# Two column blocks of a gated projection take two of their five later products together, by seven half-width products

## The chip, the cores and the metric

The kernel runs on one core of one Trainium2 chip. The metric is the device time of one execution in microseconds (us), as the median of several runs. The engines are named as in the profile: PE is TensorE, PEld its weight loads, DVE VectorE, ACT ScalarE, POOL GpSimd and SP SyncE.

## The reference

A graph network over 1024 nodes with 512 features: a graph convolution, four layers of attention and gated feed-forward, and a second graph convolution. All of it is float32. The change lies in the gated feed-forward of each layer:

```python
for i in range(L):                                   # L = 4
    a = _attn(_ln(h, ln2_w[i], ln2_b[i]), cond, Wq[i], Wk[i], Wv[i], Wo[i])
    h = h + a
    u = _ln(h, ln3_w[i], ln3_b[i]) @ geglu_w[i] + geglu_b[i]      # 512 -> 4096
    val, gate = jnp.split(u, 2, axis=-1)
    f = val * jax.nn.gelu(gate, approximate=False)                # 1024 x 2048
    h = h + f @ ffo_w[i] + ffo_b[i]                               # 2048 -> 512
```

## The kernel before

**Products by sevens.** Most matrix products are split into two by two blocks and made from seven block products instead of eight, with sums of left blocks and of right blocks formed beforehand on POOL or DVE, and sums of the results formed on DVE. The seven are numbered 0 to 6. Products 0 and 1 go into one bank of PSUM (a), product 5 into b, 6 and then 3 into c, 4 and then 2 into d. Product 3 is accumulated onto product 6 in c, and so it can begin only when DVE has read product 6 out of c; product 2 waits in the same way for the read of product 4 in d.

**The gated projection.** The 2048 hidden columns are made in four quarters, the loop over `r`. In a quarter the left side is weights (four blocks of 256 rows and 512 columns: values and gates, upper and lower half) and the right side the turned, normalised activations `ln3T` with their sums `ln3S`. The 512 hidden columns of a quarter are four column blocks of 128, `c` = 0 to 3.

- Quarters 1 to 3 use `Pair` (L1074): each of the products 0, 5, 6 and 4 is split into seven once more, for the column blocks `p` and `p + 2` together, in `InStep.seven_of` (L1012). The inner left sums `gi` and the inner right sums `gr` are made on POOL.
- Quarter 0, where the activations are only just ready, uses `Quad` (L930), one object per column block. `first` and `second` make products 0 and 1 during the end of the attention. `rest` (L956) makes the other five, 5, 6, 4, 3, 2 in this order, each as two matmuls of 128x512 (`multiply`, L298), with one DVE operation or two after each. ACT applies Gelu to both gates. The value rows `fT` follow on DVE, L975 to L978.

`geglu` (L1185) calls `rest` of the four blocks one after the other, then `beside(c)`, then `sums(c)`, which makes the left sums `fT`/`fs` of the following output projection on DVE (L1191 to L1195). `beside` issues, for c = 0 and 1, the right sums `gr` on POOL for the products 0, 5, 6, 4 of the later quarters, and for c = 2 the weight sums `wffs` of the output projection, four DVE operations (L214 to L217). After that `ffn_out` (L1215, banks `fa` to `fd`) runs the output projection, and POOL waits for the last `fs` (`geglu.last`) and makes the weight sums `ges` and the inner left sums `gi` of quarter 1.

Ahead of quarter 0 POOL adds the bias of the output projection to six of the eight row blocks of `h` (`add_bias`, L1505), behind the last sums of the activations.

The inner seven as it stands in `seven_of`, for two products side by side in one bank, each step two matmuls of 128x256 per product:

```python
product(0, a, True);   nc.scalar.copy(s1, a)
product(5, b, True);   add(halves_of(u2), b, s1)
product(6, c, True);   add(halves_of(s1), c, u2)
product(4, d, True);   add(w[1][:, :, M:], d, s1)
product(1, a, False);  nc.scalar.copy(w[0][:, :, :M], halves_of(a))
product(3, c, False);  add(w[1][:, :, :M], c, u2)
product(2, d, False);  self.last = add(w[0][:, :, M:], d, u2)
```

**What sets the order.** Each engine works off its own queue in order. A scheduler in the recording layer places the instructions of each engine by dependencies, due times and pool rooms when the program is built; `tc.issue_after` and `tc.keep_in_program_order` bind it, and `waiting_for` adds a wait. PSUM has eight banks, handed out from one pool.

Of the kernel before, what the change touches and what calls it, by code (L numbers as in the profile page):

```python
# [17 lines left out]
P = 128  # L18
# [5 lines left out]
def gnn_kernel(  # L24
# [70 lines left out]
    def t512(name, dtype=F32):  # L95
        return work.tile([P, 512], dtype, tag="t512", name=name)
# [4 lines left out]
    def slots_of(n, name):  # L101
        return [slot(f"{name}_{i}") for i in range(n)]
# [598 lines left out]
    def acc_tile(name):  # L701
        return accs.tile([P, 512], F32, tag="acc", name=name)
# [204 lines left out]
    def order7(blk, s1, s2, s4):  # L907

        return [blk[0], blk[1], s4, blk[3], s1, s2, blk[2]]
# [13 lines left out]
    def out_weights(t, l, r, wff):  # L923
        s = slots_of(2, f"wffs_{l}_{r}")
        b11, b12, b21, b22 = (wff[k][:, :, d * M:(d + 1) * M] for k in range(2) for d in range(2))
        t1, t2, t4 = (halves_of(s[i // 2][:, i % 2, :]) for i in range(3))
        sums_of_b(t, b11, b12, b21, b22, t1, t2, t4)
        return [b11, b21, b22, t4, t1, t2, b12]

    class Quad:  # L930
# [5 lines left out]
            self.cv = l * 2 * DFF // P + r * KC + c  # L936
            self.left, self.right = left, right

        def product(self, i, to, start):
            multiply(to, self.left[i], self.right[i],  # L940
                     [(self.c * P, (self.c + 1) * P, 0, 512)], start)

        def first(self):
            self.a = bank(f"ga_{self.n}")
# [9 lines left out]
            nc.scalar.activation(pre, pre, AF.Gelu, bias=gcols[:, cg:cg + 1])  # L954

        def rest(self):  # L956
            n, c, bias = self.n, self.c, gcols[:, self.cv:self.cv + 1]
# [6 lines left out]
            nc.vector.tensor_tensor(u3, pc, u2, OP.add)  # L964
            self.product(4, pd, True)
            g1 = t512(f"g1_{n}")
            nc.vector.tensor_tensor(g1, pd, u3, OP.add)
            self.gate(g1, n)
            self.product(3, pc, False)
            g0 = t512(f"g0_{n}")  # L970
            nc.vector.tensor_tensor(g0, pc, u2, OP.add)
            self.gate(g0, n)
            self.product(2, pd, False)
            v1 = acc_tile(f"gv1_{n}")
            nc.vector.scalar_tensor_tensor(v1, pd, bias, u2, OP.add, OP.add)  # L975
            f0, f1 = (self.fT[i][c // 2][:, c % 2, :] for i in range(2))
            nc.vector.tensor_tensor(f1, v1, g1, OP.mult)
            return lambda: nc.vector.scalar_tensor_tensor(f0, self.a, bias, g0, OP.add, OP.mult)  # L978

    def inner_left(t, x, s1, s2, s4):  # L980

# [5 lines left out]
    def quarters(room):  # L987
        return [room[:, k, j * M:(j + 1) * M] for k in range(2) for j in range(2)]
# [14 lines left out]
    def inner_right_of(i, right, rooms):  # L1003
        return inner_right(nc.gpsimd, *quarters(right[i]), rooms)
# [69 lines left out]
    class Pair(InStep):  # L1074
# [47 lines left out]
    class KeyPair(InStep):  # L1122
# [43 lines left out]
        def final(self, q, d):  # L1166
            nc.scalar.copy(self.to(0, q, 1), halves_of(d))

    def cond_rights(l, g):

        rooms = slots_of(4, f"kr_{l}_{g}")
        of = conds[l, g], conds[l, g + 1]
        return {i: inner_right(nc.gpsimd, *(x[i][:, k, :] for k in range(2) for x in of), quarters(room))
                for i, room in zip(INNER[0] + INNER[1], rooms)}

    def pairs_of(l, r, left, right, inner):
        fT = [slots_of(2, f"fT_{l}_{r}_{i}") for i in range(2)]
        return (fT, slots_of(3, f"fs_{l}_{r}"),
                [Pair(l, r, p, left, right, inner, fT) for p in range(2)])
# [5 lines left out]
    def geglu(quads, fT, s, begun, beside=lambda c: None):  # L1185
        def sums(c):
            k = c % 2
            a11, a12, a21, a22 = (fT[i][j][:, k, :] for i in range(2) for j in range(2))
            s1, s2, s4 = (x[:, k, :] for x in s)
            if c < 2:  # L1190
                nc.vector.tensor_tensor(a21, a11, a21, OP.subtract)  # L1191
            else:
                nc.vector.tensor_tensor(s2, a22, a21, OP.subtract)
                nc.vector.tensor_tensor(s1, s2, a11, OP.add)
                sums.last = nc.vector.tensor_tensor(s4, a12, s2, OP.subtract)  # L1195

        made = []

        def sums_of_made():
            while made:  # L1200
                sums(made.pop(0))

        for c, q in enumerate(quads):
            if begun:
                q.last = q.rest()()
                beside(c)
# [226 lines left out]
    for l in range(L):  # L1433
# [211 lines left out]
        last = l == L - 1  # L1645
        lnT = None
        kept = slot(f"kept_{l}")
        rights = {}

        for r in range(R):  # L1650
            if r:
                wff = out_weights(nc.gpsimd, l, r, raw_out)
            else:
                raw_out = load_out(l, 0)
            if r + 1 < R:
                raw = load_geglu(l, r + 1)
            beside = lambda c: None
            if r:
                fT, fS, quads = pairs_of(l, r, left, right, (lefts, rights))
            else:  # L1660
                wff = []

                rooms = slots_of(4, f"gr_{l}")
# [9 lines left out]
            fT = geglu(quads, fT, fS, not r, beside)  # L1673
            if r + 1 < R:
                raw_out = load_out(l, r + 1)
                with waiting_for(geglu.last, mybir.EngineType.Pool):
                    left = geglu_weights(l, r + 1, *raw)
                    rooms = [t512(f"gi_{l}_{r + 1}_{i}") for i in range(6)]
                    lefts = inner_lefts(left, [x[:, i * M:(i + 1) * M] for x in rooms
                                               for i in range(2)])  # L1680
                for s in range(2):
                    ffn_out(l, r, s, fT, wff, kept)
            elif last:
                w_out, base, again, dinv_row = load_last()
                with waiting_for(geglu.last, mybir.EngineType.Pool):
                    for nb in range(NB - 2, NB):
                        add_bias(nb)
                    w_out = out_weights(nc.gpsimd, L, 0, w_out)
                ffn_out(l, r, 0, fT, wff, kept)
            else:  # L1690
                lnT = [slots_of(2, f"ln2T_{l + 1}_{i}") for i in range(2)]
                projections = load_projections(l + 1, add_bias)
                ffn_out(l, r, 0, fT, wff, kept)
                ready_first(l + 1, [0, 1, 4, 5])
                ffn_out(l, r, 1, fT, wff, kept)
                turn_first(l + 1, [0, 1, 4, 5])
                left_to_turn = [2, 3, 6, 7]
                ready_first(l + 1, left_to_turn[:2])
# [144 lines left out]
```

## Time and profile before

| | |
|---|---|
| median of 3 runs | 2458.13 us (2458.05 to 2458.39) |
| profiled execution, its own time | 2458.91 us |
| its span, first to last instruction | 2457.1 us |
| PE busy | 2437.9 us, 99% of the span |
| DVE busy | 1584.0 us, 64% |
| ACT busy | 725.0 us, 30% |
| POOL busy | 920.3 us, 37% |
| granted TensorE clock, mean | 0.999 |

A row of the timeline gives the start in us from the span's start, the duration from the start of the first merged instruction to the modelled end of the last, the engine, the line, the operation, out<-in, the shape and the number of merged instructions; in brackets stands how long the engine had been idle and what ended that. The profile shows a float32 matmul as two records, so one product of two matmuls shows as x4. PE's records overlap, since matmuls are pipelined: the price of a matmul is the distance from start to start, not the duration of its row. The windows view gives busy time and count (x) of each engine in a stretch.

### The profile page before, as it was taken

The numbers are of one execution on the slowest core, as the hardware profiler recorded it, in microseconds if no ns is written. First come the engines' busy times: TensorE is split into PE (matmuls) and PEld (weight loads), VectorE is DVE, ScalarE is ACT, GpSimd is POOL, SyncE is SP. The second block draws the span as 40 slices with busy tenths as digits, with TensorE's granted clock in tenths as the row PEclk, the third lists the DMA queues.
The fourth block names the chain that finished last, engine by engine and source line by source line (L and its number), as shares of the span: only waits on it lengthen the run. The fifth ranks groups of instructions, "written<-read, shape, count | busy, mean of one in ns | idle before, by whom it ended". The sixth has DMA issues, their size and how long they took to land. (4 is left out here: it accounts for less than half of the span.)

```text
span 2457.1 us, 34452 instructions
## 1 busy us (share of the span) xinstructions
PE 2437.9 (99%) x13032; PEld 1881.7 (77%) x13032; DVE 1584.0 (64%) x3240; ACT 725.0 (30%) x1616; POOL 920.3 (37%) x1059
## 2 busy tenths in 40 slices
PE   7999999999999999999999999999999999999999
PEld 5778886677787887577787888477777888667777
DVE  9665666566676557666686557666685656666674
ACT  7323343122213334122213334222223333322230
POOL 0334433632553223533633224444524222454421
PEclk9999999999999999999999999999999999999999
DMA  6323222110212221111212222011131031111120
GB/s 180 121 69 116 91 95 69 52 35 18 103 31 78 88 70 59 35 52 35 77 56 69 78 71 76 18 52 52 35 99 69 14 125 44 61 52 52 37 93 35
DMA packets 78892, 163.50 MB, mean 67 GB/s; under 512 B 6952, under 2 KB 15472, under 8 KB 78720
## 3 DMA queue, kind: packets, MB, share of 16 engines
q1 hardware_dynamic: 76624, 155.81, 19.1%
q0 software_dynamic: 1376, 4.30, 0.5%
q8 instruction: 107, 1.75, 0.3%
q10 hardware_dynamic: 720, 1.11, 0.1%
q14 instruction: 65, 0.53, 0.1%
HBM read 138.12 MB, written 23.07 MB: 66 GB/s over the span
## 5 line engine op out<-in xcount | busy, mean ns | idle before, releaser
L221 POOL TENSOR_TENSOR ges<-wgate,wgate 128x1024 f32<-128x1024 f32 x16 | 37.7, 2355 | 443.2 <-DVE fs L1195 401.3
L797 ACT ACTIVATE pr<-sc,nmax 128x256 f32<-128x256 f32 x256 | 118.2, 471 | 85.5 <-DVE nmax L792 85.0
L298 PE MATMUL pa_v<-wv,ct 128*128 128x256 f32 x512 | 123.9, 385 | 0.0
L298 PE MATMUL fa<-wff,fT 128*128 128x256 f32 x512 | 121.6, 379 | 0.0
L298 PE MATMUL pc_v<-wv,ct 128*128 128x256 f32 x512 | 121.0, 379 | 0.0
L298 PE MATMUL pd_v<-wvs,ct 128*128 128x256 f32 x512 | 121.0, 379 | 0.0
L994 POOL TENSOR_TENSOR kr<-ct,ct 128x256 f32<-128x256 f32 x48 | 36.7, 765 | 211.8 <-DVE pr L802 207.2
L298 PEld LDWEIGHTS fa<-wff,fT 128*128 128x128 f32 x512 | 97.3, 190 | 21.8 <-issue 9.6
L1029 ACT COPY gs<-ga 128x512 f32<-128x512 f32 x48 | 27.9, 582 | 287.7 <-PE ga L1022 287.7
L298 PEld LDWEIGHTS pa_v<-wv,ct 128*128 128x128 f32 x512 | 94.9, 190 | 22.5 <-issue 9.2
L792 DVE TENSOR_REDUCE nmax<-sc 128x2 f32<-128x512 f32 x128 | 83.6, 678 | 41.2 <-PE sc L785 41.2
L298 PEld LDWEIGHTS pd_v<-wvs,ct 128*128 128x128 f32 x512 | 97.3, 190 | 13.2
L298 PEld LDWEIGHTS pc_v<-wv,ct 128*128 128x128 f32 x512 | 97.0, 190 | 13.0
L298 PE MATMUL ga<-ln3T,wval 128*128 128x512 f32 x224 | 104.4, 594 | 0.0
L1103 ACT ACTIVATE g<-g,gcols 128x512 f32<-128x512 f32 x96 | 69.3, 722 | 94.5 <-DVE g L1100 94.5
L802 DVE TENSOR_SCALAR pr<-pr,inv 128x256 f32<-128x256 f32 x256 | 78.3, 348 | 2.9
L894 POOL TENSOR_TENSOR ou<-ou 128x256 f32<-128x256 f32 x12 | 8.7, 726 | 190.5 <-DVE ou L893 127.4
L1230 DVE TENSOR_TENSOR hall<-fd,hall 128x512 f32<-128x512 f32 x64 | 44.1, 689 | 52.1 <-PE fd L298 52.1
L298 PE MATMUL gc<-ln3S,wgate 128*128 128x512 f32 x160 | 75.2, 592 | 0.0
L994 POOL TENSOR_TENSOR kr<-ct,kr 128x256 f32<-128x256 f32 x96 | 71.6, 746 | 0.9
L1230 DVE TENSOR_TENSOR hall<-fc,hall 128x512 f32<-128x512 f32 x64 | 43.9, 686 | 41.1 <-PE fc L298 41.1
L298 PEld LDWEIGHTS ga<-ln3T,wval 128*128 128x128 f32 x224 | 41.3, 190 | 35.9 <-issue 34.4
(548 smaller groups left out, 6409.3 us busy)
## 6 DMA issues: line engine op xcount, KB each, us to landing
ct<-cond_dram SPq DMA_DIRECT2D x72, 512.0 KB, 5.3
wval<-in_L_gnn_geglu_w_dram SPq DMA_DIRECT2D x32, 512.0 KB, 3.7
wgate<-in_L_gnn_geglu_w_dram SPq DMA_DIRECT2D x32, 512.0 KB, 4.5
wff<-in_L_gnn_ffo_w_dram SPq DMA_DIRECT2D x32, 512.0 KB, 3.8
cond_dram<-ct SPq DMA_DIRECT2D x24, 512.0 KB, 2.9
cond<-in_L_gnn_cond_dram SPq DMA_DIRECT2D x32, 256.0 KB, 4.8
ct<-cond_dram SPq DMA_DIRECT2D x24, 256.0 KB, 5.9
wk<-in_L_gnn_Wk_dram SPq DMA_DIRECT2D x8, 512.0 KB, 4.3
```

The source lines that it names most:

```text
L221: t.tensor_tensor(s1, a21, a22, OP.add)
L298: each(nc.tensor.matmul(at, left[:, k, l0:l1], right[:, k, r0:r1], start=start and n == 0 and k == 0, stop=n == len(cols_of) - 1 and k == ...
L792: nc.vector.tensor_reduce(nmax, ps3, AX.X, OP.max, negate=True)
L797: nc.scalar.activation(pr3[:, a, :], ps3[:, a, :], AF.Exp, bias=nmax[:, a:a + 1], accum_out=tot[:, a:a + 1])
L802: scores.last = nc.vector.tensor_scalar(pr3[:, a, :], pr3[:, a, :], inv[:, a:a + 1], None, OP.mult)
L894: t.tensor_tensor(p7, p7, u2, OP.add)
L994: t.tensor_tensor(to, of, less, OP.subtract)
L1029: nc.scalar.copy(s1, a)
L1103: nc.scalar.activation(g, g, AF.Gelu, bias=gate)
L1230: nc.vector.tensor_tensor(to, halves_of(of), to, OP.add)
```

## The change

In quarter 0 the column blocks 0 and 2 stay with `rest`, all five products one after the other. The column blocks 1 and 3 leave it. Their products 5 and 6 are made together by a new class `Late`, derived from `InStep`: the two left blocks of 128 columns each and the right blocks form a two by two split, so that `seven_of` makes the two products for both blocks from 14 matmuls of 128x256 in place of 8 of 128x512. The products 4, 3 and 2 of the blocks 1 and 3 then follow in step, 4 for both, 3 for both, 2 for both.

The sums that this needs are moved or added on POOL: four sums for each of the two left blocks (`gl`, 128x128), and the right sums `gr` for 5 and 6, which were made later under `beside`, now come ahead of the six bias additions. `beside` makes only the other two right sums, and with them the weight sums `wffs` on DVE, once, after `Late`'s inner products. The results of the inner seven are put together in `wos`, with DVE: five additions in `seven_of`, two for the term `s1` of product 0, and two that add product 5 to product 6. `gu2` and `gu3` of blocks 1 and 3, four additions, go. ACT copies twice more.

In the built program, between the end of block 2's last product and the output projection, the queues hold this, in this order (new names as in the diff; "1" and "3" are the column blocks):

- PE: the 14 narrow matmuls (inner a, b, c, d, a, c, d, two each), product 4 of 1 and of 3, product 3 of 1 and of 3, product 2 of 1 and of 3, then `fa`, `fc`, one matmul of `fd`, one of `fb`, the rest of `fd` and `fb`. Before, one matmul of `fa` stood ahead of block 3's product 3.
- DVE: `gv`, `fT`, `fT` and the first `fs` of block 2; the inner addition after b; two more `fs`; the inner additions after c, d and the second c; an `s1` term; the inner addition after the second d; one `wffs`; the other `s1` term; two `wffs`; one sum of 5 and 6; one `wffs`; the other sum of 5 and 6; the pre-gates `g1` of 1 and 3, `g0` of 1 and 3; the upper `fT` of 1 and 3; `gv` and `fT` of 1, `gv` of 3; the left sum of block 1 (`fT`); `fT` of 3; three `fs`.
- POOL: eight `gl`, then the eight `gr` of 5 and 6 with one bias addition ahead of the last of them, five bias additions, the eight `gr` of 0 and 4.

```diff
-        def product(self, i, to, start):
+        def product(self, i, to, start, each=lambda ins: ins):
...
+        def upper(self, g0):
+            f0, bias = self.fT[0][self.c // 2][:, self.c % 2, :], gcols[:, self.cv:self.cv + 1]
+            return nc.vector.scalar_tensor_tensor(f0, self.a, bias, g0, OP.add, OP.mult)
+
+        def lower(self, pd, u2, g1):
+            f1, bias = self.fT[1][self.c // 2][:, self.c % 2, :], gcols[:, self.cv:self.cv + 1]
+            v1 = acc_tile(f"gv1_{self.n}")
+            nc.vector.scalar_tensor_tensor(v1, pd, bias, u2, OP.add, OP.add)
+            nc.vector.tensor_tensor(f1, v1, g1, OP.mult)
...
+    class Late(InStep):
+        x = "g"
+        two = 5, 6
+
+        def __init__(self, l, quads):
+            self.n, self.quads = f"{l}_late", quads
+            self.w = [wos[:, 2 * q:2 * q + 2, :] for q in range(2)]
+            rooms = [t512(f"gl_{l}_{i}") for i in range(2)]
+            n = quads[0].c * P
+            self.lefts = {}
+            for i, room in zip(self.two, rooms):
+                x = quads[0].left[i]
+                blk = [x[:, k, m * M + n:m * M + n + P] for m in range(2) for k in range(2)]
+                sums = [room[:, j * P:(j + 1) * P] for j in range(3)]
+                Late.last = sums_of_a(nc.gpsimd, *blk, *sums)
+                self.lefts[i] = order7(blk, *sums)
+
+        def step(self, i, k):
+            return self.lefts[i][k], self.rights[i][k]
+
+        def rest(self, made, meanwhile):
+            *_, (p5, p6) = self.seven_of(self.two)
+            with tc.issue_after(self.last.ins):
+                meanwhile()
+            for q, x in enumerate(self.quads):
+                nc.vector.tensor_tensor(p5[q], p5[q], x.s1, OP.add)
+                nc.vector.tensor_tensor(p6[q], p6[q], p5[q], OP.add)
+            d, g1 = [], []
+            for q, x in enumerate(self.quads):
+                d.append(bank(f"gd_{x.n}"))
+                x.product(4, d[q], True, tc.keep_in_program_order)
+                g1.append(t512(f"g1_{x.n}"))
+                nc.vector.tensor_tensor(g1[q], d[q], p6[q], OP.add)
+                x.gate(g1[q], x.n)
+            for q, x in enumerate(self.quads):
+                c = bank(f"gc_{x.n}")
+                x.product(3, c, True, tc.keep_in_program_order)
+                g0 = t512(f"g0_{x.n}")
+                nc.vector.tensor_tensor(g0, c, p6[q], OP.add)
+                x.gate(g0, x.n)
+                x.upper(g0)
+            for q, x in enumerate(self.quads):
+                x.product(2, d[q], False, tc.keep_in_program_order)
+                x.lower(d[q], p5[q], g1[q])
+                made(x.c)
...
+        if late:
+            for c in (0, 2):
+                quads[c].last = quads[c].rest()
                 sums(c)
-            else:
+            late.rest(sums, beside)
+        else:
+            for q in quads:
                 q.run(sums_of_made)
...
         summed = ln3_sums(nc.vector, g)
+        rooms = slots_of(4, f"gr_{l}")
         with tc.issue_after(summed.ins):
+            late = Late(l, quads[1::2])
+        with tc.issue_after(Late.last.ins):
+            rights = {i: inner_right_of(i, right, quarters(rooms.pop(0))) for i in late.two}
+            late.rights = rights
             for nb in range(NB - 2):
                 add_bias(nb)
...
-                def beside(c):
-                    with waiting_for(quads[c].last, mybir.EngineType.Pool):
-                        if c < 2:
-                            for i in INNER[c]:
+                def beside():
+                    with waiting_for(quads[0].last, mybir.EngineType.Pool):
+                        for i in INNER[0] + INNER[1]:
+                            if i not in rights:
                                 rights[i] = inner_right_of(i, right, quarters(rooms.pop(0)))
-                    if c == 2:
-                        wff.extend(out_weights(nc.vector, l, 0, raw_out))
+                    wff.extend(out_weights(nc.vector, l, 0, raw_out))
```

More of the change, by code (lines that the diff above doesn't have):

```diff
@@ L937, in __init__ @@
             self.left, self.right = left, right
-        def product(self, i, to, start):
+        def product(self, i, to, start, each=lambda ins: ins):
             multiply(to, self.left[i], self.right[i],
-                     [(self.c * P, (self.c + 1) * P, 0, 512)], start)
+                     [(self.c * P, (self.c + 1) * P, 0, 512)], start, each)
+        def upper(self, g0):
[6 more added lines that the diff above has]
+            nc.vector.tensor_tensor(f1, v1, g1, OP.mult)
         def first(self):
@@ L956, in rest @@
         def rest(self):
-            n, c, bias = self.n, self.c, gcols[:, self.cv:self.cv + 1]
+            n = self.n
             pb, pc, pd = (bank(f"{x}_{n}") for x in ("gb", "gc", "gd"))
@@ L973, in rest @@
             self.product(2, pd, False)
[L974 to L978, printed above, removed]
+            self.lower(pd, u2, g1)
+            return self.upper(g0)
     def inner_left(t, x, s1, s2, s4):
@@ L1183, in quads_of, with geglu @@
         return fT, slots_of(3, f"fs_{l}_{r}"), [Quad(l, r, c, left, right, fT) for c in range(KC)]
-    def geglu(quads, fT, s, begun, beside=lambda c: None):
+    def geglu(quads, fT, s, late=None, beside=lambda: None):
         def sums(c):
@@ L1201, in sums_of_made @@
                 sums(made.pop(0))
[L1203 to L1206, printed above, removed]
+        if late:
+            for c in (0, 2):
+                quads[c].last = quads[c].rest()
                 sums(c)
-            else:
+            late.rest(sums, beside)
+        else:
+            for q in quads:
                 q.run(sums_of_made)
@@ L1656, in gnn_kernel @@
                 raw = load_geglu(l, r + 1)
-            beside = lambda c: None
             if r:
                 fT, fS, quads = pairs_of(l, r, left, right, (lefts, rights))
+                fT = geglu(quads, fT, fS)
             else:
                 wff = []
-                rooms = slots_of(4, f"gr_{l}")
-                def beside(c):
-                    with waiting_for(quads[c].last, mybir.EngineType.Pool):
-                        if c < 2:
-                            for i in INNER[c]:
+                def beside():
+                    with waiting_for(quads[0].last, mybir.EngineType.Pool):
+                        for i in INNER[0] + INNER[1]:
+                            if i not in rights:
                                 rights[i] = inner_right_of(i, right, quarters(rooms.pop(0)))
-                    if c == 2:
-                        wff.extend(out_weights(nc.vector, l, 0, raw_out))
-            fT = geglu(quads, fT, fS, not r, beside)
+                    wff.extend(out_weights(nc.vector, l, 0, raw_out))
+                fT = geglu(quads, fT, fS, late, beside)
             if r + 1 < R:
```

1 line of the change is left out of this document (removed).

## The prediction

> **What bounds the kernel now.** I read the page first, for the bound, and then only the stage that is rewritten.
>
> ```profile
> span 2457.1 us, 34452 instructions
> ...
> PE 2437.9 (99%) x13032; PEld 1881.7 (77%) x13032; DVE 1584.0 (64%) x3240; ACT 725.0 (30%) x1616; POOL 920.3 (37%) x1059
> ...
> PEclk9999999999999999999999999999999999999999
> ```
>
> PE is busy for all but 19.2 us of the span, at full clock throughout. So a matmul less is time gained, unless the stage then waits for another engine. The next view is the timeline of layer 0, PE alone, from the end of block 1 (442.75) into the output projection. I call 442.75 zero below.
>
> ```profile
> 442.75 1.88 PE L298 MATMUL gb<-ln3S,ges 128*128 128x512 f32 x4
> ...
> 451.33 1.88 PE L298 MATMUL gb<-ln3S,ges 128*128 128x512 f32 x4
> ...
> 456.48 0.59 PE L298 MATMUL fa<-wff,fT 128*128 128x256 f32 x2
> 456.92 1.88 PE L298 MATMUL gc<-ln3S,wgate 128*128 128x512 f32 x4
> 458.63 1.95 PE L298 MATMUL gd<-ln3T,ges 128*128 128x512 f32 x4
> 460.42 1.46 PE L298 MATMUL fa<-wff,fT 128*128 128x256 f32 x6
> 461.71 1.89 PE L298 MATMUL fc<-wff,fT 128*128 128x256 f32 x8
> 463.44 0.59 PE L298 MATMUL fd<-wffs,fs 128*128 128x256 f32 x2
> ```
>
> From 442.75 to 451.33 five products run: 8.58 / 5 = 1.716 us for one, two wide matmuls. `fc` is four narrow matmuls: 463.44 - 461.71 = 1.73, 0.432 each. There are no gaps but one: the product at 458.63 takes 460.42 - 458.63 = 1.79, 0.07 too long. The whole stretch, 442.75 to 463.44, is 20.69 us. What stops PE there is shown by the weight loads, in the timeline and, summed over the run, in the list of waits (us, times, longest):
>
> ```profile
> 458.60 0.30 PEld L298 LDWEIGHTS gd<-ln3T,ges 128*128 128x128 f32 x2 [0.63 <-DVE g L967]
> ```
>
> ```profile
> PEld gd L298 <- DVE g L967: 2.5, 4, 0.6
> ```
>
> Four waits in the run, and the projection comes four times: I work out layer 0 and multiply. DVE is already on the edge here, and the windows of blocks 0 and 1 and of this stretch tell how near:
>
> ```profile
> 425.58:442.75 17.17, 17.17 (x41) 7.60 (x40) 8.25 (x12) 2.89 (x4) 13.65 (x15) 1.00 0.00 0
> 442.75:463.44 20.69, 20.69 (x57) 10.49 (x56) 16.83 (x27) 3.48 (x5) 6.59 (x9) 1.00 0.14 41
> ```
>
> DVE works 8.25 of 17.17 us in the first and 16.83 of 20.69 us in the second, because the four `wffs` operations and the `fs` sums stand there.
>
> **The change, part by part.**
>
> *PE.* Four products (5 and 6 of two blocks) go: 4 x 1.716 = 6.86 us. Fourteen narrow matmuls come: 14 x 0.432 = 6.05. That is 0.81 us less a layer, and the 0.07 goes too, as block 3's old order is gone: 0.88, or 3.5 us over four layers, if nothing waits. That is 0.14% of the time: even whole, the gain stays within 0.2% (4.9 us), about what a measurement of this kernel can tell from no change.
>
> The row against a rule: narrow `fc` costs 0.432 and a wide matmul 0.858, just half. The Trainium skill (TensorE: Matmul & The Clock Gate, "Back-to-back issue gap") gives for sustained streams with weight loads some 81 ns at 128 columns and 131 ns at 512, so that by it narrow matmuls cost more per column than wide ones, and the exchange would lose. The trace shows no such price at 256 columns. It is kept below as a rival.
>
> *DVE.* Four additions go, nine come: 5 more in this stretch. From the rows below an operation lasts about 0.68 us, so the load is 16.83 + 5 x 0.68 = 20.2 us, while PE needs 20.69 - 0.88 = 19.8. DVE is now the fuller engine, in its own fixed order, and the time comes from walking through its queue. The timeline of DVE, behind the end of block 2 and at the end of block 3, gives the steps:
>
> ```profile
> 451.54 0.75 DVE L975 SCALAR_TENSOR_TENSOR gv<-gd,gcols,gu 128x512 f32<-128x512 f32 x1 [1.03 <-PE gd L298]
> 452.39 0.69 DVE L977 TENSOR_TENSOR fT<-gv,g 128x512 f32<-128x512 f32 x1
> 453.00 0.75 DVE L978 SCALAR_TENSOR_TENSOR fT<-ga,gcols,g 128x512 f32<-128x512 f32 x1
> 453.66 0.68 DVE L214 TENSOR_TENSOR wffs<-wff 128x512 f32<-128x512 f32 x1
> ...
> 456.06 0.68 DVE L964 TENSOR_TENSOR gu<-gc,gu 128x512 f32<-128x512 f32 x1
> ...
> 457.87 0.68 DVE L967 TENSOR_TENSOR g<-gd,gu 128x512 f32<-128x512 f32 x1
> ...
> 461.95 0.68 DVE L977 TENSOR_TENSOR fT<-gv,g 128x512 f32<-128x512 f32 x1
> 462.66 0.69 DVE L1193 TENSOR_TENSOR fs<-fT,fT 128x512 f32<-128x512 f32 x1
> 463.39 0.69 DVE L1194 TENSOR_TENSOR fs<-fs,fT 128x512 f32<-128x512 f32 x1
> 464.00 0.68 DVE L1195 TENSOR_TENSOR fs<-fT,fs 128x512 f32<-128x512 f32 x1
> ```
>
> Step to step: 0.60 behind an addition (453.66 to 456.06 is four), 0.66 behind a three-operand one (453.00 to 453.66), 0.73 if it needs the one before it (462.66 to 463.39), 0.85 if that one has three operands (451.54 to 452.39). DVE starts 0.21 after a product's nominal end (451.33 to 451.54). And PE goes on 0.16 after DVE: L967 ends at 458.55, and the product it held up ran effectively from 458.63 + 0.07 = 458.70 (458.71 with the unrounded price).
>
> *First wait.* `Late`'s second use of c needs the inner addition that reads c (its fifth step of PE done, 10 x 0.432 = 4.32). On DVE this addition is the eighth operation: `gv`, `fT`, `fT`, `fs`, the addition after b, two `fs`, then it. Block 2's end in the rows above is the same queue with other names: three operations, then five additions, and the eighth, L964, starts at 456.06, 4.73 after the product's end at 451.33. So it ends at 4.73 + 0.68 = 5.41, and PE goes on at 5.57: a stall of 1.25 us. Before, that place was harmless: `gc`'s second use stood behind `gd` and a matmul of `fa`, at 456.92. Behind the waiting matmul stands all of PE's queue. The next addition (0.73 later) frees d at 4.73 + 0.73 + 0.68 + 0.16 = 6.30, before the second c is through at 5.57 + 0.86 = 6.43. Its four banks are no further wait: the last to come free is read by block 2's second gate addition, whose Gelu starts at 450.60 in the ACT row below, before the block's end. `Late` ends at 7.30 instead of 6.05, and the six wide products at 7.30 + 10.30 = 17.60.
>
> *Second wait.* DVE's next ones follow PE: the addition after the second c at 6.43 + 0.21, a dependent one, the last inner one at about 8.0. From there eight operations at 0.60 bring the first `g1` to 12.8, three more the last `g0` to 14.6 (block 3's product 3 ends at 14.16, then 0.21). ACT has four gates in a row; the rows that price it:
>
> ```profile
> 450.60 0.72 ACT L954 ACTIVATE g<-g,gcols 128x512 f32<-128x512 f32 x1 [1.05 <-DVE g L971]
> ...
> 461.97 0.58 ACT L1236 COPY kept<-fa 128x512 f32<-128x512 f32 x1 [0.87 <-PE fa L298]
> ```
>
> At 0.72 each from 13.5 the fourth is done at 16.4; DVE's upper `fT` of 3 starts there, and behind it come `gv` (0.66), `fT` (0.85), `gv` (0.60), then the left sum of block 1 (0.66) at 19.2, done for PE at 20.0. PE is through with `fa` at 17.60 + 1.73 = 19.33 and with one matmul of `fc` at 19.76. Stall: 0.3. The first `fs` product needs the second of the three last sums, at 19.2 + 0.60 + 0.73 + 0.73 = 21.3, done for PE at 22.1; PE asks for it at 21.4 + 0.86 = 22.2: no stall. `fc` ends at 21.36 where it ended at 20.69.
>
> ACT's two added copies (0.58) lie in its gaps: it works 3.48 of 20.69 us. Uncovered they would cost 1.2.
>
> *POOL and the loads.* The sums for `Late` must be ready by zero plus 0.86.
>
> ```profile
> 425.88 7.39 POOL L1505 TENSOR_TENSOR hall<-hall,ffb 128x512 f32<-128x512 f32 x6
> ...
> 438.53 0.72 POOL L994 TENSOR_TENSOR gr<-ln3T,gr 128x256 f32<-128x256 f32 x1
> ...
> 464.81 2.35 POOL L221 TENSOR_TENSOR ges<-wgate,wgate 128x1024 f32<-128x1024 f32 x1 [14.58 <-DVE fs L1195]
> ...
> 480.76 0.72 POOL L224 TENSOR_TENSOR gi<-ges,gi 128x256 f32<-128x256 f32 x1
> ...
> 485.02 1.03 PE L1022 MATMUL gb<-gr,gi 128*128 128x256 f32 x4
> ...
> 496.25 1.88 PE L298 MATMUL ga<-ln3T,wval 128*128 128x512 f32 x4
> ```
>
> The eight `gl` are not in the trace; each lies between nothing and a `gr` at twice its size, 0.72. I take 0.4, an estimate along the line of 0.72 at 256 and 1.23 (7.39 / 6) at 512 columns. From 425.88: 3.2 + 8 x 0.72 + 1.23 = 10.2, so 436.1, with 7.5 us to spare; at 0.72 for each `gl` still 5. The bias is done by 442.3, before the output projection touches `hall`. The last sums for quarter 1 start when the last `fs` is done, at 22.6 instead of 464.68 - 442.75 = 21.9, as PE is late by the same 0.7; PE uses `gi` 3.5 us after it is made (480.76 + 0.72 to 485.02). The weight loads keep their order on SP's queue; four rooms come earlier to `gr` and later to the loads, whose data for quarter 1 is used here at 464.81 and was loaded in the attention.
>
> *The sum.* -0.81 - 0.07 + 1.25 + 0.3 = +0.67 a layer, +2.7 us in all. The profiled execution took 2458.91, 1.81 outside its span and 0.78 above the median; against its own time that makes 2461.6, against the median of 2458.13 it makes 2460.8, which I give.
>
> **The rivals.**
>
> *DVE keeps up* (faster, but within 0.2%). If the inner additions were not held up, say because the `fs` sums overlap more than the rows show, neither wait appears: 2458.13 - 3.5 = 2454.6. For it speaks that in quarter 1 the same inner seven, done twice, runs without a gap: the 26 narrow matmuls from 485.02 to 496.25 take 11.23, 0.432 each. Against it, in that place DVE has no sums of a finished block to make in between, and here its load is 20.2 us for PE's 19.8. Chance 0.14.
>
> *POOL slows DVE* (slower). While POOL sums `gr` of 0 and 4, DVE runs the chain to the first wait. One row shows an addition with both inputs in SBUF stretched as POOL starts its sums, another an unstretched one:
>
> ```profile
> 437.09 0.89 DVE L1191 TENSOR_TENSOR fT<-fT,fT 128x512 f32<-128x512 f32 x1
> ...
> 443.60 1.89 POOL L994 TENSOR_TENSOR gr<-ln3T 128x256 f32<-128x256 f32 x2 [0.81 <-DVE fT L978]
> ...
> 444.22 0.69 DVE L977 TENSOR_TENSOR fT<-gv,g 128x512 f32<-128x512 f32 x1
> ...
> 448.71 1.52 POOL L994 TENSOR_TENSOR gr<-ln3S,gr 128x256 f32<-128x256 f32 x2
> ```
>
> 0.89 - 0.68 = 0.21 on `fT` and the three `fs` ahead of the eighth operation lengthens the first wait by 0.84: +1.51 a layer, 6.0 us, 2464.2. It decides if POOL still sums at zero plus 4.7; by the working above it does, from 442.3 on for as long as those eight took, 443.60 to 450.23. The row at 444.22 speaks against. Chance 0.17. The Trainium skill (GPSIMD Engine Reference, "Key points") says that GpSimd shares its SBUF interfaces with VectorE and contends with VectorE instructions that have two SBUF inputs; the one row agrees, the other does not.
>
> *No net effect*: the waits just eat the gain, 2458.1. It needs the first wait to be half of what I find. Chance 0.06.
>
> *Narrow matmuls not half price*: between 0.432 and 0.858 each, at the worst 14 x 0.858 = 12.0 instead of 6.86, +5.1 a layer and 2478. The rows at 461.71 and 463.44 speak against; chance 0.01. This is what the page's rule on the issue gap would bring.
>
> **How the numbers follow.** Forecast 0.60, rivals 0.14, 0.17, 0.06 and 0.01, other 0.02. The first wait lies between 0 and 2.1 (with the 0.21), the second between 0 and 0.8 (every dependent step at 0.85). The forecast's own range, 0.2 to 1.3 a layer, is 2459.0 to 2463.3. The range 2457.0 to 2465.0 leaves out the first rival and the outliers. Slower by over 0.2%, above 2463.05: the second rival, the edge of the forecast (0.06), the fourth and half of the rest, 0.25. Faster by over 0.2%: 0.01, the other half, as the whole gain does not reach it. Within: 0.74.
>
> **What would show it.** A wait of PE's weight loads in `Late`'s second use of c, four times some 1.2 us, ended by DVE; the eighth DVE operation at about 4.7; a wait of about 0.3 in `fc`; DVE at 20 us in the stretch. I am wrong if PE runs through `Late` without a gap, if POOL ends PE's wait there, or if the difference lies outside quarter 0.

## The result and the profile after

The changed kernel took 2472.7 us (median of four runs, 2471.68 to 2474.2), the kernel before 2458.26 beside it: 1.0058 times as long, 95% interval 1.0045 to 1.0071. The forecast was 2460.8, with a range of 2457.0 to 2465.0. The sign was right, the size was not: +14.4 us, 0.58%, instead of +2.7.

The page of the changed kernel (profiled execution 2472.1 us):

```profile
span 2470.3 us, 34642 instructions
...
PE 2439.6 (99%) x13080; PEld 1894.4 (77%) x13080; DVE 1604.3 (65%) x3260; ACT 729.5 (30%) x1624; POOL 939.7 (38%) x1091
...
PEclk9999999999999999999999999999999999999999
```

At this grain nothing is to be seen: each digit of `PEclk` averages over 61.8 us. The timeline of layer 0 shows it, PE alone. Zero, the end of block 2, is 442.60 here.

```profile
442.60 0.59 PE L1029 MATMUL ga_late<-ln3S,ges 128*128 128x256 f32 x2
...
446.49 0.59 PE L1029 MATMUL ga_late<-ln3T,wgate 128*128 128x256 f32 x2
449.68 0.70 PE L1029 MATMUL gc_late<-gr,ges 128*128 128x256 f32 x2 [2.59 <-DVE gs_late L1033]
450.21 0.87 PE L1029 MATMUL gc_late<-gr,wgate 128*128 128x256 f32 x2
450.87 1.06 PE L1029 MATMUL gd_late<-ln3S,gl 128*128 128x256 f32 x2
451.72 1.06 PE L1029 MATMUL gd_late<-ln3T,gl 128*128 128x256 f32 x2
452.58 4.21 PE L298 MATMUL gd<-ln3S,ges 128*128 128x512 f32 x8
456.63 3.60 PE L298 MATMUL gc<-ln3S,wgate 128*128 128x512 f32 x8
460.06 3.60 PE L298 MATMUL gd<-ln3T,ges 128*128 128x512 f32 x8
463.50 1.89 PE L298 MATMUL fa<-wff,fT 128*128 128x256 f32 x8
465.22 1.89 PE L298 MATMUL fc<-wff,fT 128*128 128x256 f32 x8
466.95 0.59 PE L298 MATMUL fd<-wffs,fs 128*128 128x256 f32 x2
```

Read the starts, from row to row. The ten steps of `Late` up to 446.92 (446.49 + 0.43) cost 0.432 each, as forecast. Then PE stands for 2.76 us until 449.68. The last four narrow matmuls take 2.90 (449.68 to 452.58) instead of 1.73, and product 4 of both blocks 4.05 instead of 3.43. From 456.63 on every product has its old price, and `fc` has no wait. So 442.60 to 466.95 is 24.35 us where 20.69 stood before: -0.88 (the exchange) + 2.76 (the wait) + 1.17 + 0.62 (slow matmuls) = +3.67, 0.01 off by rounding.

The slow part is in three of the four layers: the same stretch takes 24.35, 24.36, 22.69 and 24.36 us. Together that is 13.0 us over before, and the span is 13.2 us longer. So nearly all of the loss is in this place. The wait, summed over the run (us, times, longest), has the name that was forecast:

```profile
PE gc_late L1029 <- DVE gs_late L1033: 10.4, 4, 2.6
```

**Why the wait is 2.76 and not 1.25.** The timeline of DVE over the eight operations that were counted:

```profile
442.81 0.75 DVE L950 SCALAR_TENSOR_TENSOR gv<-gd,gcols,gu 128x512 f32<-128x512 f32 x1 [1.03 <-PE gd L298]
443.66 1.21 DVE L951 TENSOR_TENSOR fT<-gv,g 128x512 f32<-128x512 f32 x1
444.80 0.74 DVE L945 SCALAR_TENSOR_TENSOR fT<-ga,gcols,g 128x512 f32<-128x512 f32 x1
445.46 1.24 DVE L1249 TENSOR_TENSOR fs<-fT,fT 128x512 f32<-128x512 f32 x1
446.62 0.68 DVE L1033 TENSOR_TENSOR gu_late<-gb_late,gs_late 128x512 f32<-128x512 f32 x1
447.22 0.68 DVE L1250 TENSOR_TENSOR fs<-fs,fT 128x512 f32<-128x512 f32 x1
447.81 1.21 DVE L1251 TENSOR_TENSOR fs<-fT,fs 128x512 f32<-128x512 f32 x1
448.94 0.68 DVE L1033 TENSOR_TENSOR gs_late<-gc_late,gu_late 128x512 f32<-128x512 f32 x1
```

It is the queue of the prediction, in its order, and `gs_late` is the eighth. But it starts 6.34 after zero, not 4.73. Three additions with both inputs in SBUF take 1.21 to 1.24 instead of 0.68: 1.62 us more. The forecast of 1.25 counted what PE loses in all. The first matmul behind the wait takes 0.10 longer also at full clock (*warm* and *pool_later* below), so 2.76 + 0.10 = 2.86 is to be set against it, and 2.86 - 1.25 = 1.61 is by how much the eighth operation is late. POOL in the same time:

```profile
442.92 1.41 POOL L1001 TENSOR_TENSOR gr<-ln3T 128x256 f32<-128x256 f32 x2
444.29 1.18 POOL L1001 TENSOR_TENSOR gr<-ln3T,gr 128x256 f32<-128x256 f32 x1
...
447.24 1.23 POOL L1001 TENSOR_TENSOR gr<-ln3S 128x256 f32<-128x256 f32 x1
448.44 1.98 POOL L1001 TENSOR_TENSOR gr<-ln3S,gr 128x256 f32<-128x256 f32 x2
```

The two take turns. DVE's `fT` starts at 443.66, POOL's pair of sums ends at 444.33, and `fT` ends 0.54 after that. POOL's next, started at 444.29, lasts 1.18 instead of 0.72 and ends 0.60 after `fT`. DVE's last `fs` ends at 449.02, 0.55 after POOL's sum that ends at 448.47. The additions that read a bank of PSUM (`gu_late`, `gs_late`, one input in SBUF) keep their 0.68. The Trainium skill (SBUF — State Buffer, "Who interferes with whom") states that a DVE instruction with two SBUF inputs and a GpSimd instruction that reads SBUF exclude each other, the later one waiting for the whole of the other; these rows agree with it.

**Why the matmuls are slow.** Windows put exactly around the low clock (us, then busy time of PE, PEld, DVE, ACT, POOL, then PEclk) show it at half:

```profile
450.40:453.81 3.41, 3.41 (x8) 2.34 (x8) 2.39 (x5) 0.00 (x0) 0.01 (x1) 0.50 0.02 5
1023.84:1027.25 3.41, 3.41 (x7) 2.04 (x7) 3.20 (x6) 0.00 (x0) 0.00 (x0) 0.50 0.00 0
1597.28:1600.69 3.41, 3.41 (x11) 1.69 (x10) 3.38 (x7) 0.00 (x0) 0.00 (x0) 1.00 0.00 0
2167.30:2170.71 3.41, 3.41 (x9) 2.70 (x9) 1.91 (x4) 0.00 (x0) 0.51 (x1) 0.50 0.00 0
```

The clock does not fall when PE stops, but 0.72, 1.15 and 0.24 us after it has gone on, and for 3.41 us each time. The starts of the falls, 450.40, 1023.84 and 2167.30, lie 573.44 and 1143.46 apart: 168.0 and 335.0 times 3.4133 us. So they lie on one grid. The windows of this grid that hold the four waits:

```profile
446.99:450.40 3.41, 0.82 (x4) 0.67 (x4) 3.31 (x5) 0.59 (x1) 3.33 (x4) 1.00 0.00 0
1020.43:1023.84 3.41, 1.14 (x5) 1.03 (x6) 2.90 (x4) 0.28 (x1) 2.93 (x3) 1.00 0.00 0
1593.87:1597.28 3.41, 1.55 (x7) 1.38 (x8) 2.88 (x5) 0.00 (x0) 2.52 (x3) 1.00 0.01 2
2163.89:2167.30 3.41, 0.80 (x4) 0.40 (x3) 3.31 (x6) 0.59 (x1) 3.33 (x4) 1.00 0.00 0
```

PE was busy for 0.82, 1.14 and 0.80 us of the window before each fall. In layer 2 a wait as long (2.62 us idle in PE's row) lies across a border of the grid, PE was busy for 1.55 us of the window that holds most of it, and the clock stayed. The kernel before had such a fall too, elsewhere, near its start, which the row of digits on its page does not show:

```profile
82.60:86.01 3.41, 1.43 (x7) 0.96 (x6) 1.05 (x7) 0.58 (x1) 0.00 (x0) 1.00 0.04 10
86.01:89.42 3.41, 3.41 (x9) 2.24 (x8) 1.79 (x7) 2.20 (x4) 0.19 (x1) 0.50 0.21 6
```

PE was busy for 1.43 us there and POOL not at all.

The Trainium skill (TensorE: Matmul & The Clock Gate, "Part 1: The HAM clock gate (the "warmup" mystery)") gives such a free-running window of 3413 ns and two clocks, whole and half: the trace agrees. Its rule for avoiding the fall (in "HAM oscillation — how this bites in real kernels"), no idle gap above some 3.4 us, is too lenient by this trace: 2.27 us of idle time within one window was enough.

### The profile page after: what moved, and what is told of

Same layout as the page of the kernel before. It is cut to its first block, busy times and chain, and to the rows that moved or that the text cites. A ratio compares the mean times of both kernels' runs of the same rounds, so it can differ in the third digit from the quotient of the medians.

```text
span 2470.3 us, 34642 instructions
## 1 busy us (share of the span) xinstructions
PE 2439.6 (99%) x13080; PEld 1894.4 (77%) x13080; DVE 1604.3 (65%) x3260; ACT 729.5 (30%) x1624; POOL 939.7 (38%) x1091
## 5 line engine op out<-in xcount | busy, mean ns | idle before, releaser
L298 PEld LDWEIGHTS pd_v<-wvs,ct 128*128 128x128 f32 x512 | 97.3, 190 | 13.2
```

Of the source, the lines that this page charges most:

```text
L298: each(nc.tensor.matmul(at, left[:, k, l0:l1], right[:, k, r0:r1], start=start and n == 0 and k == 0, stop=n == len(cols_of) - 1 and k == ...
```

## The experiments

The theories. *Contention:* POOL's sums stretch DVE's chain. *Queue:* the chain is late because block 2's three sums stand in it ahead of the addition PE waits for. *Clock:* the wait itself lowers PE's clock. Their rival is that the slow matmuls, or the wait, come from elsewhere. Runs of one group share the runs of before: 2459.17 (order, pool_later, fill, warm), 2459.16 (pool_alone, idle_3, idle_4, early), 2458.66 (idle_2, light, order_again).

### order: block 2's sums behind the pair's products

```diff
             for c in (0, 2):
                 quads[c].last = quads[c].rest()
-                sums(c)
-            late.rest(sums, beside)
+                if not c:
+                    sums(c)
+            def meanwhile():
+                sums(2)
+                beside()
+            late.rest(sums, meanwhile)
```

> The three sums of block 2 are issued behind the inner seven products instead of ahead of the addition that reads c. If their place in VectorE's queue makes the wait (theory of the queue): that addition starts at about 4.2 us after the end of block 2 instead of 6.34, TensorE's wait of 2.76 is gone, and with it the slow matmuls behind it (1.17 + 0.62); a layer then gains the 0.88 of the exchange: 2458.3 - 4 x 0.88 = 2454.7, or up to 2456 if the output projection then waits for the sums. If the queue does not matter and the wait is the inner chain's own length: unchanged, 2472.7.

2456.99 us, 0.9992 times before (0.9983 to 1.0002). PE in the place of the wait, and DVE's addition:

```profile
446.65 0.70 PE L1029 MATMUL gc_late<-gr,ges 128*128 128x256 f32 x2
...
455.91 3.70 PE L298 MATMUL gd<-ln3T,ges 128*128 128x512 f32 x8
```

```profile
443.33 1.21 DVE L951 TENSOR_TENSOR fT<-gv,g 128x512 f32<-128x512 f32 x1
...
445.91 0.69 DVE L1033 TENSOR_TENSOR gs_late<-gc_late,gu_late 128x512 f32<-128x512 f32 x1
```

The addition starts 3.63 after zero (442.28; 4.2 was expected), PE's wait is below 0.1, and the clock is 1.0 throughout. `fT` is as long as ever. So the wait hangs on the queue: with the sums of block 2 out of it, what contention is left no longer holds PE up at c. The 14.4 us are gone; whether the kernel is faster than before, the interval leaves open. Of the gain of 0.88 a layer 0.50 is left: from zero to the first matmul of quarter 1 before took 41.41 us (442.75 to 484.16), this kernel 40.91. Small waits of some 0.4 in sum remain, at c and around the last product 2 (455.91), which waits for the gates' additions.

### pool_later: POOL's sums of 0 and 4 only after the pair's products

```diff
-                    with waiting_for(quads[0].last, mybir.EngineType.Pool):
+                    with waiting_for(late.last, mybir.EngineType.Pool):
```

> GpSimd's sums of the right blocks of 0 and 4 start only when the inner products' last addition is done, so it is idle beside the chain to the wait. If GpSimd stretches VectorE's additions (theory of contention): fT and the two fs return from 1.21 to 1.24 to about 0.68, the addition that reads c starts at 4.73 and the wait is 1.25 as predicted. The time then tells when the clock falls: if it falls only after a longer idle, +0.37 a layer, 2459.8; if also after 1.25 us, some 1.8 a layer more, 2467. If the additions are long for another reason: durations and wait unchanged, 2472.7.

2471.15 us, 1.005 times before (1.0033 to 1.0067). Both numbers of the prediction for the first wait come out, and the time, expected at 2459.8 or 2467, does not. DVE's chain (zero is 442.63) and PE:

```profile
447.36 0.68 DVE L1033 TENSOR_TENSOR gs_late<-gc_late,gu_late 128x512 f32<-128x512 f32 x1
...
451.80 1.21 DVE L1204 TENSOR_TENSOR wos<-wos,gs 128x512 f32<-128x512 f32 x1
```

```profile
448.10 0.70 PE L1029 MATMUL gc_late<-gr,ges 128*128 128x256 f32 x2 [0.98 <-DVE gs_late L1033]
...
449.93 3.60 PE L298 MATMUL gd<-ln3S,ges 128*128 128x512 f32 x8
...
458.20 3.70 PE L298 MATMUL gd<-ln3T,ges 128*128 128x512 f32 x8 [1.24 <-DVE g L1211]
...
464.85 1.56 PE L298 MATMUL fc<-wff,fT 128*128 128x256 f32 x6 [0.80 <-DVE fT L1247]
```

`gs_late` starts 4.73 after zero, to the hundredth the forecast. PE goes on 1.15 late (448.10 against 442.63 + 4.32), and the four matmuls from there take 1.83 (to 449.93) instead of 1.73: 1.25 in all, as forecast. The clock stays at 1.0. But from 451.80 on five more additions of DVE run at 1.21, because POOL's sums now lie there, and two later waits appear. Contention is shown in both directions: where POOL is idle the additions take 0.68, where it sums they take 1.21. To move it is not to remove it.

### fill: product 4 into the wait

```diff
             nc.scalar.copy(w[0][:, :, :M], halves_of(a))
+            between()        # in Late: product 4 of blocks 1 and 3
             product(3, c, False)
```

> Product 4 of blocks 1 and 3 (four wide matmuls, 3.43 us) is moved between the inner second a and second c, where TensorE stood still for 2.76; VectorE's queue and GpSimd's work stay as they are. If the wait is only a matter of TensorE's order, it goes, the clock stays at 1.0 and a layer gains 0.88: 2454.7, up to 2457 if the output projection waits for VectorE's late sums. If another wait takes its place (VectorE is full: 20.2 us of work for 19.8), 2458 or more, with a wait in the output projection of above 1 us a layer.

2464.13 us, 1.002 times before (1.0011 to 1.003): the second outcome.

```profile
451.25 0.59 PE L1029 MATMUL gc_late<-gr,ges 128*128 128x256 f32 x2
...
459.19 3.70 PE L298 MATMUL gd<-ln3T,ges 128*128 128x512 f32 x8 [1.76 <-DVE g L1216]
```

The first wait is gone (the wide matmuls before 451.25 fill it). With the work that would have come later used up, PE reaches product 2 before DVE has made the gates' additions, and waits 1.76 there, not in the output projection where I had expected the next wait. The chain of DVE is as late as before, so most of the wait moves on.

### warm: discarded matmuls in the wait

```diff
             nc.scalar.copy(w[0][:, :, :M], halves_of(a))
+            between()        # three products of 128x512 into a bank that nobody reads
             product(3, c, False)
```

> Three discarded wide matmuls (2.57 us) stand in the wait between the second a and the second c; nothing else changes, VectorE's chain is as late as before. If the slow matmuls behind the wait come from the idle time (theory of the clock), they return to 0.43 and 0.86 and a layer saves 1.17 + 0.62: 2472.7 - 7.2 = 2465.5. If they are slow for another reason, the time stays at 2472.7.

2467.74 us, 1.0037 times before (1.0022 to 1.0051): 8.6 over its own before, where the changed kernel was 14.4 over.

```profile
447.00 2.74 PE L1206 MATMUL gw_late<-ln3S,ges 128*128 128x512 f32 x6
449.74 0.70 PE L1029 MATMUL gc_late<-gr,ges 128*128 128x256 f32 x2
...
451.57 3.60 PE L298 MATMUL gd<-ln3S,ges 128*128 128x512 f32 x8
```

The second c starts 7.06 after zero, as in the changed kernel (7.08). But the four narrow matmuls take 1.83 instead of 2.90, and product 4 is back at 3.43. The stretch is 22.65 in all four layers, which is what layer 2 of the changed kernel took. So the slow matmuls come from PE's idle time: with work in it, the clock stays. A fall costs 24.35 - 22.65 = 1.7 us, half of 3.41; 0.10 of the 1.17 counted above stays also at full clock (1.83 against 1.73). The kernel saved 5.8, not the 7.2 expected: in the profiled execution of the changed kernel only three layers fell, which makes 5.1.

### pool_alone: POOL's part of the change without the pair

```diff
-            for c in (0, 2):
-                quads[c].last = quads[c].rest()
-                sums(c)
-            late.rest(sums, beside)
+            for c, q in enumerate(quads):
+                q.last = q.rest()
+                if c == 2:
+                    beside()
+                sums(c)
```

> GpSimd's part of the change alone: it makes gl (whose result is not used here) and the right sums of 5 and 6 ahead of the biases, and those of 0 and 4 behind block 0; TensorE and VectorE compute all four blocks one by one as before. If the loss lies in the stage of the pair (both theories): as before, 2458 to 2460, no wait of TensorE over 0.7 us in the quarter. If GpSimd's new order costs by itself: towards 2472.

2458.94 us, 1.0001 times before (0.9991 to 1.001). The sums for `gl` overwrite columns of the gate's operands that block 3 here still reads in its products 5 and 6, so this kernel computes something else, by the same operations on PE and DVE as before. POOL's new order by itself shows no cost; the loss needs the pair.

### idle_2, idle_3, idle_4: the wait made by other means

Kernel *order* with two, three or four copies on DVE ahead of the addition that reads c:

```diff
             add(halves_of(u2), b, s1)
+            for _ in range(3 if two == (5, 6) else 0):
+                nc.vector.tensor_copy(u2, u2)
             product(6, c, True)
```

> The kernel 'order' (no wait of TensorE) with three discarded copies on VectorE between the inner addition that reads b and the one that reads c: TensorE must wait some 2.0 us there, GpSimd's work does not matter. Theory of the clock's windows (the clock falls at times that lie on a grid of 3.41 us, if more than about 2.0 us of the window before are idle; in the changed kernel 2.27 and more did, 1.86 did not): it falls in none or few of the four layers. Theory that any wait of over about 2 us drops it: in all four or in none. Time without a fall 2456.5 + 4 x 2.0 = 2464.5, and 1.7 more for each fall.

> As idle_3 with four copies: TensorE waits some 2.7 us, as long as in the changed kernel, but with VectorE's copies and not GpSimd's sums as the cause. Theory of the windows: falls in those layers where more than about 2.0 us of the wait lie in one window of the grid, some two to four of the four, each with 3.4 us at half clock and 1.7 us of loss. If the falls came from GpSimd's or VectorE's work and not from the wait, none. 2456.5 + 4 x 2.7 = 2467.3, and 1.7 for each fall.

> As idle_3 with two copies on VectorE, at the 0.87 each that idle_3 and idle_4 showed: TensorE waits some 1.9 us, of which its rows show 1.75 idle. Theory of the windows: as every wait with 2.22 us or more of idle time in one window of the grid was followed by a fall, and the one with 1.86 was not, the clock stays at 1.0 in all four layers: 2457.0 + 4 x 1.75 = 2464. If any wait of this kind lowers the clock: 1.7 more for each, up to 2471.

One run each. idle_3: 2474.61 us; I had put the copies at about 0.7 us, but three took 2.68, so PE's rows show up to 2.61 idle and not 2.0, and the clock fell in all four layers. That is what the theory of any wait over about 2 us also says: idle_3 and idle_4 do not part the two. idle_4: 2478.93, idle 3.45, falls in all four. idle_2, sized with the measured copies: 2464.38 where 2464 was expected, 1.74 idle, no fall. The falls start at 450.24, 1023.68, 1597.12 and 2170.56 in idle_3, each 168.0 times 3.4133 us after the one before, and at 450.18, 1027.04, 1600.48 and 2173.92 in idle_4, 169.0, 168.0 and 168.0 times. What speaks for windows is the grid, on which all eleven falls in this stage lie, in three executions, and layer 2 of the changed kernel, where a wait of 2.62 us idle was followed by no fall. PE was busy for 0.81 to 1.19 us of the window before each fall in idle_3. Windows of idle_4, layer 0:

```profile
446.77:450.18 3.41, 0.77 (x4) 0.34 (x2) 3.27 (x4) 0.59 (x1) 3.01 (x4) 1.00 0.00 0
450.18:453.59 3.41, 2.60 (x6) 2.15 (x7) 1.88 (x3) 0.00 (x0) 0.00 (x0) 0.50 0.00 0
453.59:457.00 3.41, 3.41 (x6) 1.71 (x6) 3.08 (x6) 0.00 (x0) 0.00 (x0) 0.50 0.02 5
```

Here the fall lasts two windows: 2.60 us of work in the first did not bring the clock back, 3.41 in the second did. The step down lies between 1.19 and 1.55 us of work in a window, at 35 to 45%. Whether DVE is busy with sums or with copies makes no difference, and the fall of the kernel before came with POOL idle. Windows elsewhere in the traces put the step closer: the 1.43 us of the kernel before, above, were followed by a fall; the 1.42 us of this window at the end of *early* were not, the clock of the next window is 1.00:

```profile
2449.41:2452.82 3.41, 1.42 (x7) 0.92 (x5) 1.61 (x3) 0.00 (x0) 0.00 (x0) 1.00 0.70 266
```

So the step lies near 1.4 us. Whether it is one fixed share everywhere stays open: the ends of matmuls are modelled, and 1.42 and 1.43 stand the wrong way round.

### early and light: clear POOL, then unload DVE

early is *order* with all four right sums made ahead of the pair, without a wait, and the biases behind the first output projection. light is *early* with the `wffs` sums on POOL:

```diff
-            rights = {i: inner_right_of(...) for i in late.two}
+            rights = {i: inner_right_of(...) for i in late.two + INNER[0][:1] + INNER[1][1:]}
...
-            for nb in range(NB - 2):
-                add_bias(nb)
...
+                if not r:            # behind ffn_out of quarter 0
+                    for nb in range(NB - 2):
+                        add_bias(nb)
...
-                    wff.extend(out_weights(nc.vector, l, 0, raw_out))
+                    wff.extend(out_weights(nc.gpsimd, l, 0, raw_out))     # light alone
```

> The kernel 'order', with all four right sums made by GpSimd ahead of the pair and without a wait, and the six bias additions moved behind the first output projection, so that GpSimd is idle while VectorE works through the chain. Theory of contention: fT returns from 1.21 to 0.68 and what is left of the waits in 'order' (0.39 us a layer by the trace) shrinks to 0 to 0.2: 2458.3 - 4 x 0.7 to 0.88 = 2454.8 to 2455.5. If the biases in their new place hold VectorE up in quarter 1 or the last sums for quarter 1 come too late: 2457 or more.

> The kernel 'early' with the four wffs operations made by GpSimd, behind its right sums, instead of VectorE, which then has 20.2 - 4 x 0.6 = 17.8 us of work in the stretch for TensorE's 19.8. If what was left of the waits in 'early' (the gates' additions come 0.4 us late in the products behind the fours) is VectorE's load: the waits go and a layer gains the whole 0.88, 2455.7 against a before of 2459.2 (3.5 less). If it is the order or the Gelus: as 'order', 2457. If GpSimd's sums stretch VectorE's again: 2458 or more.

> The same kernel as 'order', timed beside 'light' on one chip: 2457.0 where before is 2459.2, some 2.0 less, as its trace shows 0.5 a layer less between block 2's end and quarter 1.

early: 2460.01 us, 1.0 times before (0.9991 to 1.0009). The contention is gone as expected (`fT` 0.69) and so is the wait at c, but zero to quarter 1 is 40.97, no better than 40.91 of *order* and above the 2454.8 to 2455.5 expected: what was left only moved to the gates. Its eleven times fall into two groups, 2456.62 to 2458.15 and 2460.01 to 2460.71; the traced one (2457.0) is of the lower. The mean granted clock is 0.999 in all six of the upper group and 1.000 in four of the five of the lower, so falls of the clock elsewhere may make the upper; no trace of an upper one was kept, and it stays open.

light: 2455.66 us, 0.9987 times before (0.9978 to 0.9996), faster than both kernels: 3.0 less than its own before, where 3.5 was expected. order_again beside it: 2457.21, 0.9993 (0.9984 to 1.0002). The windows of light, from zero to the first matmul of `fd`:

```profile
443.05:462.85 19.80, 19.80 (x70) 12.95 (x69) 17.94 (x28) 4.43 (x7) 4.16 (x3) 1.00 0.17 53
```

The stretch is 19.80 where before had 20.69 and the prediction's exchange without waits gives 19.81. DVE's load is 17.94 for 19.80. The gates' additions, for which product 2 waits, in *early* and in *light*:

```profile
455.65 1.28 DVE L1211 TENSOR_TENSOR g<-gd,wos 128x512 f32<-128x512 f32 x2
```

```profile
453.97 1.28 DVE L1211 TENSOR_TENSOR g<-gd,wos 128x512 f32<-128x512 f32 x2
```

They start 13.33 after zero (442.32) in *early* and 10.92 (443.05) in *light*: 2.41 earlier, the four `wffs` operations at 0.60. So what *early* had left was DVE's load, and the exchange is worth its whole 0.88 once DVE has room: from zero to quarter 1 *light* takes 40.51, 0.90 less than before.

## Why the prediction was wrong

**PE, -0.88 a layer:** right. The narrow matmuls cost 0.432, and light shows the whole sum.

**First wait:** right in place, cause, count and row, wrong in size. The eighth operation came 6.34 after zero instead of 4.73, because three additions lay beside POOL's sums and took 1.21 to 1.24. The step that failed is the price of DVE's queue: I walked through it as if POOL stood idle, though POOL's sums were known to run then. I took the row at 444.22, where DVE was not stretched, against the row that was, and gave the stretching a chance of 0.17 as a rival. With POOL out of the way the forecast is exact (pool_later: 4.73, and 1.25 lost). The rival itself was mis-sized: it took 0.21 on four operations, measured were 0.53 to 0.56 on three, since an addition waits for the rest of POOL's instruction. The prediction's own rows showed the turn-taking, with POOL as the loser: two sums took 1.89 at 443.60 and 1.52 at 448.71. By these rows the one that starts later loses, and the change shifted who that is.

**What was missing altogether:** a fall of the clock. The prediction read full clock throughout and priced the matmuls behind a wait as those before. The reading was wrong in itself: it came from a row whose digits average over 61 us, and in the same trace the clock stood at 0.50 from 86.01 to 89.42, behind a pause of PE. Three falls of 1.7 us are 5.1 of the 13.2 us by which the profiled execution is longer. At the forecast wait of 1.25 it would not have come (pool_later, and idle_2 at 1.74), so this term follows from the first one's size.

**Second wait, +0.3 in `fc`:** not in the changed kernel, where PE came later still and `fc` runs through. The mechanism was real: in pool_later `fc` waits 0.80 for the left sum of block 1, the operation named.

**POOL, ACT and loads at nothing:** right for POOL's deadlines (the last sum for `Late` was made at 436.4 by the trace, 436.1 was forecast) and for ACT; wrong in that POOL's sums have a price for DVE. The POOL part alone shows no cost (pool_alone).

**DVE as the fuller engine:** the prediction's 20.2 us for 19.8 was the right warning. In the changed kernel it works 21.93 of the stretch's 24.35 us; order and early reach only half of the gain by their traces, and light, with four operations fewer, all of it.

## What to carry to other kernels

When a change gives DVE a chain that PE waits for, look at each operation of the chain for two SBUF inputs and at what POOL does beside it: then the price is what is left of POOL's instruction, here 0.53 to 0.56 us on an addition of 0.68. Order the queue so that what PE waits for comes first, and bring the total load of that engine under PE's time, or the wait only moves. And price a wait of PE twice: if it leaves PE idle for more than about 2 us of a 3.41 us window, the work behind it runs at half clock for the next window, and in one case here for two.

## What the runs showed of the hardware

- PE's clock steps between 1.0 and 0.5 at times on a grid of 3.4133 us that runs through the whole execution. In this stage a window with 1.19 us of PE work or less was followed by a fall, one with 1.55 us was not (elsewhere 1.43 was and 1.42 was not); 2.60 us of work in a window at half clock did not end it. The fall can come after the wait is over, and the same wait costs 1.7 us more or not, by where it lies on the grid (24.36 or 22.69 for one stretch).
- A DVE addition of 128x512 with both inputs in SBUF took 0.68 alone and 1.21 to 1.24 beside POOL sums of 128x256, which themselves went from 0.72 to 1.18 and 1.23. Additions with one input in PSUM kept 0.68.
